# Rotary attention gated by a mixture-scaled sign layer: scales, weight sums and the first loads in another order

## The chip, the core and the metric

The kernel runs on one core of a Trainium2 chip. The core has five engines with queues of their own: TensorE (PE in the profile, with its weight loads apart as PEld), VectorE (DVE), ScalarE (ACT), GpSimd (POOL) and SyncE (SP), which here does nothing but issue transfers. They meet at semaphores. Matmul results land in PSUM, everything else lies in SBUF. The metric is the device time of one execution in microseconds (us), the median of the runs; all tensors are float32.

## What is computed

Cut to what matters (B = 4 sequences of S = 512 tokens, E = 1024, 16 heads of 64, NE = 8 experts):

```python
xn = layernorm(x)                                   # over E, eps 1e-5
q, k, v = xn @ Wq, xn @ Wk, xn @ Wv                 # rotary on q and k
attn = softmax(mask(q @ k.T) / 8)                   # causal
s = (attn @ v) @ Wo
routing = softmax(xn @ gate_w.T)                    # (tokens, 8)
in_scale = routing @ in_channel_scale               # (8, 1024)
out_scale = routing @ out_channel_scale
f = ((xn * in_scale) @ sign(weight).T) * out_scale + bias
out = x + s * silu(f)
```

The two channel scales are tables of 8 rows and 1024 columns. The kernel multiplies them by the routing on TensorE in the format float32r, with each value split into a high part (rounded to float32r) and a low part (the value less the high part). Partition rows of the tables `isc` and `osc` hold groups of eight experts; of each 16 rows eight keep the high part and eight the low part.

## The kernel before

**Stages.** Normalized x is transposed into `X[b]` (features on partitions), one sequence at a time. The projections run in 16 slots, one for each sequence b and group g of four heads (`project`, three matrices m = 0, 1, 2 for q, k, v). Each projection is a Strassen-Winograd product: seven block products in place of eight, over sums and differences of the weight (`form_w`, S1 to S4, VectorE, line 253) and of x (`form_x`, T1 to T4, line 265). A slot is 84 steps of `project`, some 28 for each m. Between these steps the attention of the group before is interleaved in pieces: transposes of the probabilities (`transpose_p`, into `pT`), `scores_1`, `scores_3`, `scores_02`, and `values` (product with v). After the slots come the sign layer (`ffn`, line 874), with which the last attention units are interleaved, and the output projection (`project_out`, line 994), again with a Strassen form. Its sums of the weight Wo (`sum_wo`, line 865) are made once, while the first two `ffn` groups run: t1 to t4, each in four pieces c.

**Order.** TensorE runs in the order in which the program is written (`manual_schedule` for PE). VectorE and ScalarE are in written order in the beginning only (the loop over four tiles, lines 693 to 719); elsewhere a planner orders each engine's queue at compile time by when it reckons that inputs are there.[...] `tc.keep_in_program_order` pins an instruction behind the instruction that was written last for its engine ahead of it; others may still be put between. SP's transfers are in a planned order as well, and all go through one queue.

**Beginning.** Four tiles of x (512 KB each, `load_x`) and the first weight in two halves (`load_half_w`, 512 KB each) are loaded in the order tile 0, tile 1, half 0, tile 2, tile 3, half 1. For each tile VectorE takes statistics (line 179), ScalarE the deviation (187), VectorE the reciprocal and the normalized tile (194, 195), TensorE transposes (209). TensorE runs filler transposes (`keep_warm`, line 669) while it waits. The statistics of tile t + 1 stand ahead of the normalization of tile t in VectorE's queue.

**Interleaving.** `interleave` runs the pieces of a slot evenly over the 84 steps. In slot 0 there is no attention yet; its nine pieces are the three steps of the router (`router`: logits, softmax, transposed result `rt` at line 547), the loads of the scales, their splitting, and empty ones:

```python
            while done * len(pieces) < (n + 1) * n_fill:
                next(fill, None)
                done += 1
```

**Scales.** `load_scales` fills the 128 rows of a tile by 16 transfers of the same eight rows (line 563). `split_scales` makes `is_high` from a mask (568, 569), rounds the tile on ScalarE (572), subtracts on VectorE (573), clears the low part where the row is a high one (574), and puts both together (575). The two tiles come from the pool `xin`, whose two buffers take the tiles of the next sequence afterwards (line 169).

**The end of the attention.** The last two units u0 and u1 are transposed in three steps each, with a step of `ffn` after each (`dense`), and then multiplied by v (`values`). `dense(gates, 5)` takes a weight sum after each of its steps; two more are taken after each `values`. PSUM banks for all of this come from one ring of four (`bank`).

Of the kernel before, what the change touches and what calls it, by code (L numbers as in the profile page):

```python
# [9 lines left out]
F32 = mybir.dt.float32  # L10
F32R = mybir.dt.float32r
AF = mybir.ActivationFunctionType
ALU = mybir.AluOpType
AX = mybir.AxisListType
# [8 lines left out]
NE = 8  # L23
P = 128
# [21 lines left out]
def t_place(h, j):  # L46

    return [(h, 0), (2 + h, 0), (4, 256 * h), (2 + h, 384)][j]
# [3 lines left out]
def attn_gated_ffn_kernel(  # L52
# [14 lines left out]
    nc = tc.nc  # L67
# [3 lines left out]
    cp = ctx.enter_context(tc.tile_pool(name="const", bufs=1))  # L71
# [9 lines left out]
        out=mask,  # L81
        in_=mask,
# [17 lines left out]
    isc = cp.tile([P, E], F32R, name="isc")  # L100
    osc = cp.tile([P, E], F32R, name="osc")

    high = cp.tile([P, 8], F32, name="high")
    nc.gpsimd.memset(high, 1.0)
    for sign, base in ((1, 0), (-1, 7)):
        nc.gpsimd.affine_select(
            out=high,
            in_=high,
# [3 lines left out]
            pattern=[[-16 * sign, 8]],  # L112
            channel_multiplier=sign,
        )
    is_high = cp.tile([P, 2], F32, name="is_high")

# [34 lines left out]
    def bank(name):  # L153
        return ring.tile([P, S], F32, tag="r", name=name)
# [9 lines left out]
    def load_x(b, t):  # L164
        if b == 0:
            xt = X1[:, t, :]
        else:
            xt = xip.tile([P, E], F32, tag="x", name=f"x_{b}_{t}")
        nc.sync.dma_start(out=xt, in_=x[(b * TPB + t) * P : (b * TPB + t + 1) * P, :])
        xin[b, t] = xt  # L170
# [26 lines left out]
    def layernorm(b, t):  # L197
        half_statistics(b, t, 0)
        half_statistics(b, t, 1)
        deviation(b, t)  # L200
        normalize(b, t)
# [274 lines left out]
    def values(u):  # L476
        b, g, i = u
        pr = g + NGRP * i
        pv = bank("pv_%d_%d_%d" % u)
        for j in range(TPB):  # L480
            for h in range(2):
                r = h * D
                n, o = t_place(h, j)
                nc.tensor.matmul(  # L484
                    pv[r : r + D, j * P :],
                    lhsT=V[u][:, j, r : r + D],
                    rhs=PT[u][:, n, o : o + (TPB - j) * P],
                    start=(j == 0),
                    stop=(j == TPB - 1),
                )  # L490
        at = atp.tile([P, S], F32, tag="at", name="at_%d_%d_%d" % u)
        nc.vector.tensor_copy(at, pv)
        nc.sync.dma_start(
            out=at_d[b].rearrange("t p (c q) -> p t c q", c=NC)[:, :, pr, :],
            in_=at.rearrange("p (t q) -> p t q", t=TPB),
        )
# [54 lines left out]
                nc.sync.dma_start(out=rt_d[b, t], in_=rT[32 * t : 32 * t + 32, :])  # L551


    staged, scales = {}, []

    def load_sign(n):
        staged[n] = xip.tile([P, E], F32, tag="x", name=f"wb_{n}")
# [1 line left out]

    def load_scales(src):  # L560
        v = xip.tile([P, E], F32, tag="x", name="scales")
        for t in range(P // NE):
            nc.sync.dma_start(out=v[NE * t : NE * (t + 1), :], in_=src)
        scales.append(v)

    def split_scales(dst):
        v = scales.pop(0)
        nc.vector.tensor_reduce(is_high[:, 0:1], high, AX.X, ALU.max)
        nc.vector.tensor_scalar(
            is_high[:, 1:2], is_high[:, 0:1], -1.0, 1.0, op0=ALU.mult, op1=ALU.add  # L570
        )
        nc.scalar.copy(dst, v)
        nc.vector.tensor_tensor(v, v, dst.bitcast(F32), op=ALU.subtract)
        nc.vector.tensor_scalar(v, v, is_high[:, 1:2], None, op0=ALU.mult)
        nc.vector.scalar_tensor_tensor(
            dst, dst.bitcast(F32), is_high[:, 0:1], v, op0=ALU.mult, op1=ALU.add
        )

    def make_sign(n):
# [97 lines left out]
    def load_half_w(i):  # L677
        nc.sync.dma_start(
            out=W[0, 0, 0][:, i].rearrange("p c n -> p (c n)"), in_=wqkv[0, 0][:, i * E : (i + 1) * E]
        )  # L680

    load_half_w(0)
    load_x(0, 2)
    load_x(0, 3)
    load_half_w(1)
    nc.sync.dma_start(out=gw[:, :, :NE], in_=gate_wT.rearrange("(c p) e -> p c e", p=P))
# [34 lines left out]
    def attention_pieces(k, late):  # L721

        units = [(*groups[k], i) for i in range(2)]
        w, v = late

        def pt(u):
            return [lambda n=n: transpose_p(u, n) for n in range(5)] if u else []

        def with_values(scores_of, u):
            def both():  # L730
                scores_of(units)
                if u:
                    values(u)

            return both

        def wait():
            pass

        pieces = [  # L740
            *pt(w),
            with_values(scores_1, w),
            *pt(v),
            with_values(scores_3, v),
            wait,
            lambda: scores_02(units),
            wait,
            wait,
        ]
        return pieces, units  # L750
# [12 lines left out]
    for k, (b, g) in enumerate(groups):  # L763
        pieces = []
        if k > 0:
            pieces, late = attention_pieces(k - 1, late)
        extra = []
        if g == 0:
            routing = [lambda n=n: router(b, n) for n in range(3)]
            if k == 0:  # L770
                nothing = lambda: None
                pieces = [
                    routing[0],
                    lambda: (load_scales(in_scale), load_scales(out_scale)),
                    routing[1],
                    nothing,
                    routing[2],
                    nothing,
                    lambda: split_scales(isc),
                    lambda: split_scales(osc),  # L780
                    nothing,
                ]
            else:

                pieces.insert(7, routing[0])
                pieces.insert(10, routing[1])
                pieces.insert(13, routing[2])
        elif g == 1 and b + 1 < B:
            for t in range(2):
                load_x(b + 1, t)  # L790
        elif g > 1 and b + 1 < B:
            t0 = 2 * (g - 2)
            for t in range(t0, t0 + 2):
                layernorm(b + 1, t)
            extra = [
                lambda t=t, h=h: transpose_x(b + 1, t, h) for t in range(t0, t0 + 2) for h in range(2)
            ]
            if g == 2:
                extra.append(lambda: [load_x(b + 1, t) for t in (2, 3)])

        step = max(1, (len(pieces) + len(extra)) // (len(extra) + 1))
        for n, e in enumerate(extra):
            pieces.insert(min(len(pieces), (n + 1) * step + n), e)
        if k in (4, 8, 12, 13):
            n = {4: 0, 8: 2, 12: 4, 13: 6}[k]
            pieces.insert(8, lambda: make_sign(n + 1))
            pieces.insert(4, lambda: make_sign(n))
            pieces.insert(0, lambda: (load_sign(n), load_sign(n + 1)))
        if b == B - 1:

            if g < 2:
                load_xn(g)
            if g in (1, 2):
                pieces.insert(3, lambda: in_scales(g - 1, score_banks))
            if g == 3:
                z_place[0] = [xip.tile([P, E], F32, tag="x", name=f"z0_{i}") for i in range(2)]
                pieces.insert(3, lambda: out_scales(0, score_banks))
        fill = project(b, g) if k else first
        interleave(pieces, fill, 3 * 7 * 4)
        if g == NGRP - 1 and b + 1 < B:  # L820
            for n in (3, 1, 2, 4):
                form_x(b + 1, n)
# [17 lines left out]
    for f, k in ((0, 1), (0, 0), (1, 1), (1, 0)):  # L840
        w = wop.tile([P, 4, HALF], F32, name=f"wo{f}{k}")
        for n in range(2):
            nc.sync.dma_start(
                out=w[:, 2 * n : 2 * n + 2, :].rearrange("p c n -> p (c n)"), in_=wo[k, 2 * f + n]
# [12 lines left out]
    def sum_wo(n, c):  # L857
        out_, x0, x1 = {
            1: (t1, b12, b11),
            2: (t2, b22, t1),  # L860
            3: (t3, b22, b12),
            4: (t4, b21, t2),
        }[n]
        tc.keep_in_program_order(
            nc.vector.tensor_tensor(out_[:, c, :], x0[:, c, :], x1[:, c, :], op=ALU.subtract)
        )
# [45 lines left out]
    u0, u1 = units = [(*groups[-1], i) for i in range(2)]  # L912
    w, v = late
    sums = iter([(n, c) for n in (1, 3) for c in range(4)])

    def dense(gates, n):
        for _ in range(n):
            next(gates)
            if n > 1:
                nxt = next(sums, None)  # L920
                if nxt:
                    sum_wo(*nxt)
# [7 lines left out]
    gates = gated(0)  # L930
# [13 lines left out]
    split(1, 1)  # L944
    scores_02(units)
    gates = gated(1)
    dense(gates, 5)

    sums = iter([(n, c) for n in (2, 4) for c in range(4)])
    dense(gates, 5)  # L950
    for u in units:
        for ns in ((0, 1), (2, 3), (4,)):
            for n in ns:
                transpose_p(u, n)
            dense(gates, 1)
        values(u)
        for nxt in [next(sums, None) for _ in range(2)]:
            if nxt:
                sum_wo(*nxt)
    for _ in gates:  # L960
        pass
    actx.close()
# [190 lines left out]
```

## Time and profile before

| | |
|---|---|
| time, median of 3 runs | 1192.41 us (1191.88 to 1192.67) |
| profiled execution: time | 1192.43 us |
| profiled execution: span | 1190.7 us |
| mean granted TensorE clock | 0.997 |
| HBM read, written | 95.45 MB, 25.43 MB: 102 GB/s over the span |
| first slot ends | about 54.5 us |
| last projection slot ends | about 842 us |
| output projection begins | 898.8 us |

The span runs from the first to the last instruction that the profile shows. A row of waits names the waiting engine, tile and line, then what ended the wait. In a timeline row, the brackets give the engine's idle time just before the instruction and what ended it. The chain is followed back from the last instruction to what released each step. In the windows the columns are length, busy time and instructions of PE, PEld, DVE, ACT and POOL, then the granted TensorE clock (1.00 is full), the busy share of the DMA engines and their GB/s.

### The profile page before, as it was taken

How to read it: one execution, taken by the hardware profiler on the slowest of the kernel's cores; microseconds unless marked ns; L12 is line 12 of the kernel's file. 1: busy time of each engine (PE TensorE's matmuls, PEld its weight loads, DVE VectorE, ACT ScalarE, POOL GpSimd, SP SyncE). 2: the span in 40 equal slices, each digit the busy share in tenths (PEclk: the TensorE clock that was granted, in tenths of full speed). 3: DMA queues.
4: the chain of work that ended last, by engine and by line, in shares of the span. 5: the costliest groups of instructions: out<-in, count | busy, mean ns of one | idle time of the engine just before them, and what ended most of it. 6: DMA issues, size and time to landing. Idle time of an engine off the chain costs nothing.

```text
span 1190.7 us, 17943 instructions
## 1 busy us (share of the span) xinstructions
PE 1174.0 (99%) x6760; PEld 895.1 (75%) x6760; DVE 760.6 (64%) x1397; ACT 492.3 (41%) x1133; POOL 536.5 (45%) x597
## 2 busy tenths in 40 slices
PE   8989999999999999999999999999999999999998
PEld 7869788888878888887978888887774456645664
DVE  7667676875767686576768677666865533453343
ACT  2534646443564645455463544446532121222120
POOL 0453436353433635343453544255465445544544
PEclk9989999999999999999999999999999999999999
DMA  8422432421133242223235222210504523432320
GB/s 286 142 63 72 133 107 80 151 83 56 70 115 116 89 133 72 74 81 115 85 120 203 65 80 80 80 50 18 210 9 145 194 77 107 146 102 79 107 71 35
DMA packets 60246, 122.04 MB, mean 102 GB/s; under 512 B 5248, under 2 KB 40832, under 8 KB 54144
## 3 DMA queue, kind: packets, MB, share of 16 engines
q1 hardware_dynamic: 55296, 112.11, 29.0%
q0 software_dynamic: 4576, 8.39, 2.0%
q8 instruction: 53, 0.87, 0.3%
q10 hardware_dynamic: 288, 0.39, 0.1%
q14 instruction: 33, 0.27, 0.1%
HBM read 95.45 MB, written 25.43 MB: 102 GB/s over the span
## 4 chain that ended last, share of the span: by engine, by line
PE 94%; DVE 3%; ACT 1%; DMA 1%; issue 0%; POOL 0%; SPq 0%; ACTq 0%; DVEq 0%
PE pj L304 33%; PE wo L994 16%; PE pj L312 16%; PE ff L874 9%; PE sc L402 6%; PE pv L484 6%; PE ptp L468 6%; PE xtp L209 1%; DVE nmx L417 1%; ACT p L420 1%; PE lg L506 1%; DMA x<-in_x 1%; DVE sc L413 0%; PE os L652 0%; PE is L624 0%
## 5 line engine op out<-in xcount | busy, mean ns | idle before, releaser
L430 POOL TENSOR_SCALAR p<-p,rs 128x128 f32<-128x128 f32 (+3 forms) x256 | 167.9, 669 | 182.5 <-DVE rs L428 182.5
L420 ACT ACTIVATE p<-sc,nmx 128x128 f32<-128x128 f32 (+3 forms) x256 | 132.8, 524 | 163.1 <-DVE nmx L417 160.6
L304 PE MATMUL pj<-T,S 128*128 128x256 f32 x768 | 185.0, 384 | 6.1 <-DVE S L253 6.1
L304 PEld LDWEIGHTS pj<-T,S 128*128 128x128 f32 x768 | 141.3, 192 | 25.0 <-issue 7.7
L366 POOL TENSOR_TENSOR part<-part,part 128x256 f32<-128x256 f32 x48 | 35.0, 728 | 211.4 <-ACT part L365 181.3
L276 POOL TENSOR_TENSOR sw<-sw,sin_sb 128x512 f32<-128x512 f32 x64 | 85.6, 1337 | 90.2 <-ACT sw L274 90.2
L304 PE MATMUL pj<-X,w 128*128 128x256 f32 x512 | 123.0, 381 | 0.2 <-ACT X L215 0.2
L474 ACT COPY pT<-ptp 128x512 f32<-128x512 f32 x96 | 56.2, 586 | 125.6 <-PE ptp L468 125.0
L417 DVE TENSOR_REDUCE nmx<-sc 128x2 f32<-128x512 f32 (+3 forms) x128 | 103.5, 819 | 2.6
L874 PE MATMUL ff<-sg,hi 128*128 128x512 f32 x256 | 103.3, 404 | 0.0
L304 PEld LDWEIGHTS pj<-X,w 128*128 128x128 f32 x512 | 92.7, 190 | 12.1 <-issue 1.1
L874 PE MATMUL ff<-sg,lo 128*128 128x512 f32 x256 | 99.9, 390 | 0.0
L253 DVE TENSOR_TENSOR S<-w 128x512 f32<-128x512 f32 x96 | 78.4, 818 | 30.8 <-PE pj L304 27.0
L468 PE MATMUL ptp<-ident,p 128*128 128x128 f32 x640 | 94.9, 273 | 3.0 <-DVE pT L472 1.6
L312 PE MATMUL pj<-S,T 128*128 128x128 f32 x768 | 92.9, 277 | 0.0
L273 ACT ACTIVATE sw<-c 32x512 f32<-32x512 f32 x128 | 80.4, 628 | 30.0 <-DVE c L331 28.0
L468 PEld LDWEIGHTS ptp<-ident,p 128*128 128x128 f32 x640 | 78.6, 141 | 18.1 <-DVE pT L472 2.0
L312 PEld LDWEIGHTS pj<-S,T 128*128 128x128 f32 x768 | 88.3, 192 | 2.2 <-issue 0.5
L277 POOL TENSOR_TENSOR rot<-rot,sw 128x512 f32<-128x512 f32 x64 | 83.0, 1297 | 4.9
L402 PE MATMUL sc<-rot,rot 64*128 64x384 f32 (+3 forms) x512 | 82.0, 449 | 0.0
L274 ACT ACTIVATE sw<-c 32x512 f32<-32x512 f32 x128 | 80.4, 628 | 1.8
L484 PE MATMUL pv<-pT,v 128*64 128x256 f32 (+3 forms) x512 | 76.0, 439 | 0.0
(141 smaller groups left out, 1997.6 us busy)
## 6 DMA issues: line engine op xcount, KB each, us to landing
w<-in_wqkv SPq DMA_DIRECT2D x47, 1024.0 KB
x<-in_x SPq DMA_DIRECT2D x16, 512.0 KB
xn_d<-X SPq DMA_DIRECT2D x16, 512.0 KB
at_d<-at SPq DMA_DIRECT2D x32, 256.0 KB
xp<-xn_d SPq DMA_DIRECT2D x16, 512.0 KB
ap<-at_d SPq DMA_DIRECT2D x16, 512.0 KB
xr<-in_x SPq DMA_DIRECT2D x16, 512.0 KB
wb<-in_wb SPq DMA_DIRECT2D x8, 512.0 KB
```

Source lines behind the costliest of these rows:

```text
L276: nc.gpsimd.tensor_tensor(sw, sw, sin_sb, op=ALU.mult)
L277: nc.gpsimd.tensor_tensor(rot, rot, sw, op=ALU.add)
L304: nc.tensor.matmul(ps, lhsT=wq[:, k, :], rhs=xq[:, k, :], start=(k == 0), stop=(k == 3))
L312: nc.tensor.matmul(ps[:, j * P : (j + 1) * P], lhsT=xq[:, k, j * P : (j + 1) * P], rhs=wq[:, k, :], start=(k == 0), stop=(k == 3),)
L402: nc.tensor.matmul(ps[:, h, :], lhsT=Q[u][r : r + D, i * P : (i + 1) * P], rhs=K[u][r : r + D, : (i + 1) * P], start=True, stop=True,)
L417: nc.vector.tensor_reduce(nmx, ps, AX.X, ALU.max, negate=True)
L420: nc.scalar.activation(pt[:, h, :], ps[:, h, :], AF.Exp, bias=nmx[:, h : h + 1], accum_out=ssum[:, h : h + 1],)
L430: nc.gpsimd.tensor_scalar(pt[:, h, :], pt[:, h, :], rs[:, h : h + 1], 1.0, op0=ALU.mult, op1=ALU.mult,)
L468: nc.tensor.transpose(tp[:, k, :], probs(u, i)[:, h, j * P : (j + 1) * P], ident)
L484: nc.tensor.matmul(pv[r : r + D, j * P :], lhsT=V[u][:, j, r : r + D], rhs=PT[u][:, n, o : o + (TPB - j) * P], start=(j == 0), stop=(j == ...
L874: nc.tensor.matmul(acc, lhsT=part[q, i][:, c, :], rhs=sg[4 * k + c // 2][:, (c % 2) * HALF : (c % 2 + 1) * HALF], start=(c == 0 and part i ...
L994: nc.tensor.matmul(ps, lhsT=lhs[:, k, :], rhs=rhs[:, k, :], start=(k == 0), stop=(k == 3))
```

## The change

Four edits that don't depend on one another:

1. The host repeats the eight rows 16 times, so that each scale is one transfer of 512 KB. The split is done on VectorE alone, all of it pinned: a copy that rounds, a multiplication by the low mask, and one operation `dst * sign + v` with sign +1 on high rows and -1 on low ones. The masks are made once. In slot 0 the splits move from pieces 7 and 8 to pieces 4 and 6, each behind a step of the router (counted from 1).
2. Tile 2 of the first sequence is loaded ahead of the first half weight.
3. A slot with more than 18 pieces gets one empty piece at its end (before the pieces for sign weights are put in).
4. The sums t2 and t4 of Wo leave the second `dense` and the places after `values`: three pieces of t2 go between the transposes of u1, the last piece of t2 and all of t4 behind the values of u1.

```diff
-    is_high = cp.tile([P, 2], F32, name="is_high")
+    row_kind = cp.tile([P, 3], F32, name="row_kind")
...
-    staged, scales = {}, []
+    staged, scales, scales_done = {}, [], []
...
     def load_scales(src):
         v = xip.tile([P, E], F32, tag="x", name="scales")
-        for t in range(P // NE):
-            nc.sync.dma_start(out=v[NE * t : NE * (t + 1), :], in_=src)
+        nc.sync.dma_start(out=v, in_=src)
         scales.append(v)
 
     def split_scales(dst):
         v = scales.pop(0)
-        nc.vector.tensor_reduce(is_high[:, 0:1], high, AX.X, ALU.max)
-        nc.vector.tensor_scalar(
-            is_high[:, 1:2], is_high[:, 0:1], -1.0, 1.0, op0=ALU.mult, op1=ALU.add
-        )
-        nc.scalar.copy(dst, v)
-        nc.vector.tensor_tensor(v, v, dst.bitcast(F32), op=ALU.subtract)
-        nc.vector.tensor_scalar(v, v, is_high[:, 1:2], None, op0=ALU.mult)
-        nc.vector.scalar_tensor_tensor(
-            dst, dst.bitcast(F32), is_high[:, 0:1], v, op0=ALU.mult, op1=ALU.add
+        h, low, sign = (row_kind[:, n : n + 1] for n in range(3))
+        pin = tc.keep_in_program_order
+        if not scales_done:
+            pin(nc.vector.tensor_reduce(h, high, AX.X, ALU.max))
+            pin(nc.vector.tensor_scalar(low, h, -1.0, 1.0, op0=ALU.mult, op1=ALU.add))
+            pin(nc.vector.tensor_scalar(sign, h, 2.0, -1.0, op0=ALU.mult, op1=ALU.add))
+        scales_done.append(dst)
+
+        pin(nc.vector.tensor_copy(dst, v))
+        pin(nc.vector.tensor_scalar(v, v, low, None, op0=ALU.mult))
+        pin(
+            nc.vector.scalar_tensor_tensor(
+                dst, dst.bitcast(F32), sign, v, op0=ALU.mult, op1=ALU.add
+            )
         )
...
+    load_x(0, 2)
     load_half_w(0)
-    load_x(0, 2)
     load_x(0, 3)
     load_half_w(1)
...
                     routing[0],
                     lambda: (load_scales(in_scale), load_scales(out_scale)),
                     routing[1],
+                    lambda: split_scales(isc),
+                    routing[2],
+                    lambda: split_scales(osc),
                     nothing,
-                    routing[2],
                     nothing,
-                    lambda: split_scales(isc),
-                    lambda: split_scales(osc),
                     nothing,
...
             pieces.insert(min(len(pieces), (n + 1) * step + n), e)
+        if len(pieces) > 18:
+
+            pieces.append(lambda: None)
         if k in (4, 8, 12, 13):
...
     gates = gated(1)
-    dense(gates, 5)
-
-    sums = iter([(n, c) for n in (2, 4) for c in range(4)])
-    dense(gates, 5)
+    dense(gates, 10)
     for u in units:
         for ns in ((0, 1), (2, 3), (4,)):
             for n in ns:
                 transpose_p(u, n)
             dense(gates, 1)
+            if u == u1:
+                sum_wo(2, ns[0] // 2)
         values(u)
-        for nxt in [next(sums, None) for _ in range(2)]:
-            if nxt:
-                sum_wo(*nxt)
+    sum_wo(2, 3)
+    for c in range(4):
+        sum_wo(4, c)
     for _ in gates:
...
-        "in_scale": np.ascontiguousarray(a["in_channel_scale"]),
-        "out_scale": np.ascontiguousarray(a["out_channel_scale"]),
+        "in_scale": np.tile(a["in_channel_scale"], (P // NE, 1)),
+        "out_scale": np.tile(a["out_channel_scale"], (P // NE, 1)),
```

## The prediction, made before the result was known

> **What bounds the kernel now.** I read the page's busy rows first, then TensorE's own waits, then the chain that ended last around the longest of them, then windows for the granted clock.
>
> The page, busy time and share of the span:
>
> ```profile
> PE 1174.0 (99%) x6760; PEld 895.1 (75%) x6760; DVE 760.6 (64%) x1397; ACT 492.3 (41%) x1133; POOL 536.5 (45%) x597
> ```
>
> TensorE (PE) is the bound: 16.7 us of the 1190.7 us span are left beside it, and its order is written by hand, so a microsecond in which it stands still is a microsecond of the kernel. No other edit can pay than one that takes away such a stop or a slow clock. TensorE's waits (us in total, times, longest):
>
> ```profile
> PE pj L304 <- DVE S L253: 6.1, 1, 6.1
> PE ptp L468 <- DVE pT L472: 1.6, 1, 1.6
> PE idle L669 <- POOL ident masks.py:199: 1.5, 1, 1.5
> PE xtp L209 <- DVE x L195: 1.3, 2, 1.0
> PE ptp L468 <- POOL p L430: 1.0, 2, 0.5
> ```
>
> One wait of 6.1 us stands out. The chain of waits in order of time (start, us, what) shows what made it:
>
> ```profile
> 60.18 0.94 ACT osc L572
> 61.15 1.34 DVE scales L573
> 62.52 0.76 DVE scales L574
> 63.31 1.28 DVE osc L575
> 64.59 0.61 DVE S L253
> 65.20 0.14 issue
> 65.34 5.04 PE pj L304 x12
> 70.38 1.92 PE sc L402 x8
> ```
>
> The form S3 of group (0,1) needs 0.6 us of VectorE, but stands in its queue behind the split of `osc`, which waits for ScalarE's cast. The transfer isn't to blame: weight 0,1,0 was issued at 33.71, and the DMA rate falls from 377 to 29 GB/s by 38. TensorE stands from 59.20 to 65.34, and then its twelve matmuls take 5.04 us; at full clock twelve take 2.60 (the chain has eight of them in 1.73 wherever it is undisturbed). The windows give the clock (column after the five engines):
>
> ```profile
> 62.00:64.00 2.00, 0.00 (x0) 0.00 (x0) 1.93 (x3) 0.00 (x0) 2.00 (x5) 0.75 0.20 33
> 64.00:66.00 2.00, 0.66 (x2) 0.60 (x3) 1.97 (x4) 0.00 (x0) 1.99 (x4) 0.50 0.40 70
> 66.00:68.00 2.00, 2.00 (x6) 1.58 (x5) 1.55 (x3) 0.00 (x0) 0.00 (x0) 0.50 0.82 277
> 68.00:70.00 2.00, 2.00 (x7) 1.58 (x5) 0.69 (x1) 0.00 (x0) 0.00 (x0) 0.54 0.08 14
> ```
>
> So the stall costs 6.14 us and a half clock after it: 4.97 (65.34 to the scores' 70.31) - 2.60 = 2.37. Together **8.51 us**.
>
> **Part by part. Scales.** 32 transfers of 32 KB become two of 512 KB: the same bytes, 30 issues fewer on SP. In before these fill SP's queue from 20.63 to 33.60, and weight 0,1,0 goes out directly after, at 33.71; it can now go a few us sooner. The two big transfers stand behind a queue that is full until about 24.5 (over 300 GB/s until there) and add at most 1 MB, about 3 us at that rate, so I estimate both landed by 28; the first split comes at about 32 and the second at 41.5 (below). Hidden, with 4 us or more of cover; without it, VectorE stands on the transfer.
>
> The split loses its ScalarE cast (1.04 each) and the subtraction (1.23 and 1.33), and gains a VectorE copy and one tiny operation. The copy isn't in the trace. Its lower end is the scalar multiply of the same tile, 0.75; its upper end that row's other instance, 1.64. The whole split is 0.75 + 0.75 + 1.28 = 2.8 us without and 1.64 + 1.64 + 1.96 = 5.2 with GpSimd beside it; the first has 0.45 of tiny operations more.[...] 1.64 at 49.81, while GpSimd ran `sw` and `rot`, 0.75 at 62.52.[...] I use the row, 5.2, as the worst.
>
> Where do they stand? The interleaving puts the first split at step 36 of 84 (four products into m = 1, behind the first `rot`s on VectorE, 32.1 in before's time) and the second at step 55 (behind c[1] at 41.5). TensorE's next needs of VectorE are the router's `rt` at 37.39 (1.4 us of tiny operations before it) and a bank at about 40. At 3.2: 32.1 + 3.2 + 1.4 = 36.7, in time; with GpSimd[...] (its rows run from 34.08) 32.1 + 5.7 + 1.4 = 39.2, a stop of 1.8. Part of the split is over before 34.08, so I take nothing, 1.8 as the end. The second split moves the `rot`s from 43.03 to about 46; their GpSimd addition of the last pair ran at 50.98 and the scores at 54.49, so it is covered. Before's first split already held VectorE from 48.55 to 53.67 while TensorE ran 12.50 us of `pj` L312 without a stop: cover of that kind exists.
>
> What comes after the stall goes? With no split behind 56, S3 needs only its weight and u3, both there by 51 without the split. In the next slot the same form ran at 99.20, eleven us ahead of its product at 109.86. If the planner leaves S3 behind the second reciprocal (60.22, there was no more than that ahead of the split), TensorE waits until about 61.15, 1.95 us, and not long enough for the clock: the 1.57 us wait at 886 left it at 1.00. I take zero.
>
> [...] the row has 4.97 us at half, 2.37. I take the row.
>
> **The third tile.** The beginning runs on the input's arrival:
>
> ```profile
> 2.20 7.52 DMA x<-in_x
> 9.75 0.69 DVE bn L179
> ...
> 11.50 0.64 PE xtp L209 x4
> ```
>
> Tile 2 lands at 9.72 behind half a weight; VectorE waits 1.10 for it, and normalizing tile 1 stands behind that. One 512 KB transfer ahead less, at 400 GB/s of these windows, is 1.3 us: landed at about 8.4, when VectorE comes free. Also the two `is_high` operations (6.56 to 6.89), now pinned in the split, leave the queue ahead of the first reciprocal: 0.25. VectorE ends tile 1 at 10.13, TensorE is through its fourteen fillers at 10.23, so the transposes start at 10.25, not 11.50: **1.25 us**, all of it kept down the chain (xtp, copy, pj, deviation, xtp, lg, pj at 20.63 all hang on it). The half weight lands at 9.7 instead; its product then starts at 11.55 (12.80), so 1.8 us of cover. Tile 3 and the second half are in the same place of the queue (estimate 11.1 and 12.5), asked for at 10.9 and 13.6. Ends: 0.8 if tile 2 comes at 8.85, 1.35.
>
> **The extra piece.** Lists of over 18 pieces (groups 2, 3, 4, 6, 7, 8, 10, 11, 12: nine slots) get an empty one at the end, so later pieces come some three steps of 0.43 us sooner, 1.3 us. The two 0.5 us waits on `p` L430 (265.12, 476.38) are the first transposes behind groups 4 and 8; their chain from the scores at 257.57 to GpSimd's end moves 1.3 ahead: **1.0 us**. It costs VectorE and ScalarE nothing in instructions; last copies of `pT` end 2.1 (117.15 against 119.25) and 2.9 us ahead of their `pv`, more than the step or two lost.
>
> **Weight sums.** Five L865 subtractions leave the stretch 879 to 887. There (start, us, VectorE and PE):
>
> ```profile
> 885.15 1.76 DVE L865 TENSOR_TENSOR z_t<-wo,xp 128x512 f32<-128x512 f32 x1
> ...
> 886.84 1.28 DVE L472 COPY pT<-ptp 128x512 f32<-128x512 f32 x2
> 887.57 0.66 PE L468 MATMUL ptp<-ident,p 128*128 128x128 f32 x4 [1.57 <-DVE pT L472]
> ```
>
> The copies come next after z_t (883.85), two us sooner: **1.57 us**. The sums go behind the last transposes: three singles of 0.68 between them, and five at the end, 3.4 us behind `at` (899.51 in before). VectorE was idle from 900.8 to 906.06 there, 5.3; `t2` is needed at 905.79, `t4` at 916.09. Covered; if GpSimd stretched all five to 1.76, 8.8 us would push the first `c` L1004 some 3, and TensorE has three more banks before it waits.
>
> **Sum.** 8.51 + 1.25 + 1.0 + 1.57 = 12.33. The profiled execution took 1192.43 (span 1190.7), the median is 1192.41: the same. 1192.4 - 12.3 = **1180.1 us**.
>
> **Rivals.** (a) S3 stays behind the second reciprocal: 1.95 back, 1182.1. For: in before it stood behind everything of that stretch. Against: the next slot. (b) The first split holds the router: 1.8 back, 1181.9[...]. For: GpSimd's rows at 34 to 39.7. Against: it starts before them. (c) The beginning is held by tile 3 or the half weight: nothing of 1.25, 1181.4. (d) The change doesn't do what it says: the planner still holds the form behind work that late, and 8.5 stays: 1188.6. (e) **Slower**: the squeezed pieces bring transposes onto banks whose copies wait behind ScalarE's four `sw` copies (0.63 each), one stop in each of nine slots. At the size of the one such stop in the trace, 1.57, that is 14.1, 1180.1 + 1.0 + 14.1 = 1195.2; it decides from 1.26 us a slot (11.3 / 9). Against: no such stop in any of these slots now, 2.1 us of slack.
>
> **Numbers.** Forecast 0.62, (a) 0.13, (b) 0.12, (c) 0.07, (d) 0.02, (e) 0.04. The range 1178.3 to 1185: below, the upper ends (1.35, the 0.2 and 0.3 of other small waits) and half a us of spread; above, (a), (b) and (c) two at a time. It leaves out (d), (e) and the end of (b), under 1 in 10 by these chances; the rest is room for a new order of the planner that no row shows. 0.2% (2.4 us) is about what a measurement of this kernel can tell from no change. Faster 0.95, within 0.01, slower 0.04.
>
> **What would show it.** Right: no wait on S L253 and a clock of 1.00 from 55 to 75; `xtp` for tile 1 at about 10.25; no `ptp` waits on POOL p; no wait at `pT` L472 near the end. Wrong: a wait of `rt` L547 or `pj` on VectorE at 35 to 45, or TensorE waits repeated in the nine slots.

## The result, and the profile after

| | before | after |
|---|---|---|
| median of 4 runs, us | 1192.54 (1191.88 to 1192.91) | 1179.76 (1179.35 to 1180.39) |
| ratio to before, 95% interval | | 0.9894 [0.9877, 0.9911] |
| profiled execution: time, span | 1192.43, 1190.7 | 1179.35, 1177.6 |
| mean granted TensorE clock | 0.997 | 0.999 |

The time fell by 12.8 us in the medians and by 13.1 in the profiled executions; 12.3 was predicted. The busy row of the page after, and TensorE's longest waits (us in total, times, longest):

```profile
PE 1170.6 (99%) x6760; PEld 893.5 (76%) x6760; DVE 754.0 (64%) x1396; ACT 489.3 (42%) x1131; POOL 535.4 (45%) x597
```

```profile
PE idle L673 <- POOL ident masks.py:199: 1.5, 1, 1.5
PE ptp L468 <- DVE v L331: 0.3, 1, 0.3
PE xtp L209 <- DVE x L195: 0.3, 1, 0.3
PE pj L304 <- ACT X L215: 0.2, 1, 0.2
PE rt L547 <- DVE rex L543: 0.2, 1, 0.2
```

The waits on `S` L253, on `pT` L472 and on `p` L430 are gone, and with them all that was longer than 0.3 us behind the start. One entry is new: the router's `rt`, 0.2. The same stretch as the half clock of before, in the windows after:

```profile
55.00:60.00 5.00, 5.00 (x25) 4.41 (x24) 2.68 (x7) 2.31 (x9) 0.93 (x2) 1.00 0.21 90
60.00:65.00 5.00, 5.00 (x23) 3.16 (x22) 3.78 (x5) 1.13 (x3) 1.36 (x2) 1.00 0.00 2
65.00:70.00 5.00, 5.00 (x25) 4.41 (x24) 3.56 (x9) 2.13 (x7) 4.29 (x5) 1.00 0.30 77
```

TensorE is busy throughout, and the clock (behind the five engines) is 1.00. The form S3 that it had waited for now runs at about 46.6.

Where the time came from is read best from starts: take the same instruction in both traces, and see by how much it is earlier. That lead grows in four places and shrinks in one.

| place | lead, from and to | step, us | predicted |
|---|---|---|---|
| beginning (`pj` at 20.63 before, 19.37 after) | 0 to 1.26 | 1.26 | 1.25 |
| router's `rt` | 1.26 to 0.82 | -0.44 | 0 |
| stall and half clock in slot 1 | 0.82 to 9.40 | 8.58 | 8.51 |
| the two stops on `p` | 9.40 to 10.83 | 1.43 | 1.0 |
| end of the attention | 10.89 to 13.06 | 2.17 | 1.57 |

The sum is 13.0. The last unit's end after, VectorE's rows (start, us, line, operation):

```profile
879.52 0.69 DVE L472 COPY pT<-ptp 128x512 f32<-128x512 f32 x1 [0.38 <-PE ptp L468]
880.13 0.68 DVE L872 TENSOR_TENSOR xp<-wo,xp 128x512 f32<-128x512 f32 x1
881.26 0.69 DVE L472 COPY pT<-ptp 128x512 f32<-128x512 f32 x1 [0.45 <-PE ptp L468]
...
888.47 2.49 DVE L872 TENSOR_TENSOR z_t<-wo,xp 128x512 f32<-128x512 f32 x4
893.00 0.69 DVE L1010 TENSOR_TENSOR c<-wo,part 128x512 f32<-128x512 f32 x1 [2.04 <-PE wo L1000]
```

Each copy of `pT` now waits for its transposes, not they for it. The single sums (L872; the third runs at 884.27) come behind the copies, and those moved to the end are through 2.04 us before the first result of the output projection is there.

### The profile page after: what moved, and what is told of

Its sections match the earlier page's. It is cut to its first block, busy times and chain, and to the rows that moved or that the text cites. A ratio compares the mean times of both kernels' runs of the same rounds, so it can differ in the third digit from the quotient of the medians.

```text
span 1177.6 us, 17904 instructions
## 1 busy us (share of the span) xinstructions
PE 1170.6 (99%) x6760; PEld 893.5 (76%) x6760; DVE 754.0 (64%) x1396; ACT 489.3 (42%) x1131; POOL 535.4 (45%) x597
## 4 chain that ended last, share of the span: by engine, by line
PE 98%; DVE 1%; ACT 0%; issue 0%; POOL 0%; DVEq 0%; ACTq 0%; POOLq 0%
PE pj L304 33%; PE pj L312 17%; PE wo L1000 16%; PE ff L881 10%; PE sc L402 7%; PE pv L484 6%; PE ptp L468 6%; PE xtp L209 1%; PE idle L673 1%; PE lg L506 1%; PE os L656 0%; PE is L628 0%; DVE z_t L1025 0%; DVE nmx L417 0%; ACT p L420 0%
## 5 line engine op out<-in xcount | busy, mean ns | idle before, releaser
L430 POOL TENSOR_SCALAR p<-p,rs 128x128 f32<-128x128 f32 (+3 forms) x256 | 167.4, 667 | 212.9 <-DVE rs L428 194.7
L304 PE MATMUL pj<-T,S 128*128 128x256 f32 x768 | 182.3, 380 | 0.0
L253 DVE TENSOR_TENSOR S<-w 128x512 f32<-128x512 f32 x96 | 77.4, 806 | 27.4 <-PE pj L304 23.9
```

Of the source, the lines that this page charges most:

```text
L304: nc.tensor.matmul(ps, lhsT=wq[:, k, :], rhs=xq[:, k, :], start=(k == 0), stop=(k == 3))
L430: nc.gpsimd.tensor_scalar(pt[:, h, :], pt[:, h, :], rs[:, h : h + 1], 1.0, op0=ALU.mult, op1=ALU.mult,)
```

## The experiments

Twelve kernels ran. The names b_ are the kernel before with one part added, the names a_ the changed kernel with one part taken back or altered. The kernel before was run beside each lot, with medians of 1192.29, 1192.12 and 1192.48.

| kernel | median, us (lowest to highest) | ratio to before, 95% interval |
|---|---|---|
| b_one_transfer | 1190.26 (1187.89 to 1191.56) | 0.9982 [0.9976, 0.9989] |
| b_vector_split | 1187.92 (1187.57 to 1188.04) | 0.9962 [0.9947, 0.9977] |
| b_early_pieces | 1192.07 (1191.52 to 1193.67) | 0.9999 [0.9990, 1.0007] |
| b_pinned | 1187.42 (1186.44 to 1188.17) | 0.9958 [0.9943, 0.9972] |
| a_old_tile_order | 1180.29 (1180.29 to 1180.90) | 0.9902 [0.9886, 0.9919] |
| a_no_piece | 1181.51 (1181.12 to 1182.25) | 0.9911 [0.9897, 0.9926] |
| a_old_sums | 1182.74 (1181.91 to 1182.98) | 0.9920 [0.9905, 0.9935] |
| a_splits_behind_router | 1179.90 (1179.67 to 1180.31) | 0.9898 [0.9883, 0.9912] |
| a_32_fillers | 1179.00 (1179.00 to 1179.06) | 0.9889 [0.9874, 0.9904] |
| a_22_fillers | 1178.99 (1178.84 to 1180.25) | 0.9891 [0.9876, 0.9906] |
| a_32_old_tile_order | 1180.29 (1179.97 to 1180.52) | 0.9900 [0.9884, 0.9917] |
| a_late_places | 1180.21 (1179.88 to 1180.64) | 0.9899 [0.9885, 0.9914] |

### Which part of the first edit removes the stall

**One transfer alone.**

```diff
-        for t in range(P // NE):
-            nc.sync.dma_start(out=v[NE * t : NE * (t + 1), :], in_=src)
+        nc.sync.dma_start(out=v, in_=src)
```

> Before, with each scale in one transfer and nothing else changed: the split keeps its cast on ScalarE and its late pieces. Theory P (the planner reckons 32 transfers ahead of weight 0,1,0 and so puts the form S3 late in VectorE's queue; their number alone decides): the 6.1 us wait on S L253 and the half clock go, 8.5 us, 1184.0 us. Rival S (the split's late place and its cast hold the form): the wait stays, 1192.5 us. Rival T (the weight itself comes late behind the 32 issues): also 1184.0 us.

The wait on `S` L253 is gone, but 2.0 us were gained and not eight. TensorE's longest wait, and the chain of waits of this kernel (start, us, what):

```profile
PE rt L547 <- DVE is_high L567: 4.2, 1, 4.2
```

```profile
21.04 6.77 DMA scales<-in_out_scale
27.81 0.02 issue
27.83 0.04 ACT osc L571
27.88 0.91 issue
28.79 0.37 ACT part L365
...
33.07 1.13 DVE scales L572
34.21 0.09 DVE rrs L530
34.30 1.17 DVE isc L574
35.47 1.21 DVE rex L531
...
37.01 1.00 DVE rhi L536
...
38.61 1.27 DVE rex L539 x2
...
40.30 0.83 DVE rex L543
...
41.28 0.45 PE rt L547
```

The planner put the split, which nothing pins here, well ahead: VectorE's part of the first one, at 48.55 to 53.67 before, now lies between 27.9 and 35.5. ScalarE stood on the transfer of the second scale until 27.83, ahead of `part` that VectorE needed, and VectorE's part of both splits lay between the router's operations. So the router's last operations came at 35.4 to 41.1, while GpSimd ran four operations for the rotary (34.63 to 41.09). The router's took 1.21, 1.00, 1.27 (a pair) and 0.83 us here, 4.3 together; before they had taken 0.8 together and been through by 33.4, ahead of GpSimd's rows. That stretch of 3.5 us is most of the wait: TensorE stood 4.2 us for `rt`, and from 40 to 45 the clock was 0.50. The stall was moved, not removed.

The twenty runs of this kernel differ by 3.7 us, and their mean clock from 0.996 to 1.000. The fastest, 1187.89, is the only one at 1.000. Only one of them has a trace.

**The split on VectorE alone**, pinned, with 32 transfers and the late pieces:

```diff
-        nc.scalar.copy(dst, v)
-        nc.vector.tensor_tensor(v, v, dst.bitcast(F32), op=ALU.subtract)
...
+        pin(nc.vector.tensor_copy(dst, v))
+        pin(nc.vector.tensor_scalar(v, v, low, None, op0=ALU.mult))
```

> Before, with the split on VectorE alone and pinned, but 32 transfers and the late pieces. P: the form still stands behind the second reciprocal of the next slot's scores, but no longer behind the split: a wait of 1.5 to 2.0 us on S L253[...] (1.00 throughout), some 6.5 us faster than before with 0.25 from the beginning: 1186 us. S: no wait at all, 1183.8 us. T: the wait stays about 6 us, 1192.5 us.

TensorE's wait is what rival (a) of the prediction said, and the windows show that the clock fell all the same (they are cut where the clock changed, at 62.02 and 65.43):

```profile
PE pj L304 <- DVE S L253: 1.9, 1, 1.9
```

```profile
58.61:62.01 3.40, 1.49 (x8) 1.02 (x7) 2.31 (x5) 1.28 (x5) 2.03 (x4) 1.00 0.00 0
62.02:65.42 3.40, 3.40 (x9) 2.41 (x8) 3.40 (x5) 0.00 (x0) 3.40 (x6) 0.50 0.13 22
65.43:68.84 3.41, 3.41 (x15) 1.74 (x14) 3.14 (x6) 0.11 (x1) 1.81 (x4) 1.00 0.84 202
```

S3 stood directly behind the second reciprocal, ahead of the late `osc` split. The stop ended at 61.24 and the half clock began at 62.02; the twelve matmuls took 4.60 us in place of 2.60, so 1.9 us of stop cost 3.9. This is less than the 8.5 of before by 4.6, and the time fell by 4.4.

**The places alone.**

```diff
                     routing[1],
-                    nothing,
+                    lambda: split_scales(isc),
                     routing[2],
-                    nothing,
-                    lambda: split_scales(isc),
                     lambda: split_scales(osc),
+                    nothing,
+                    nothing,
```

> Before, with only the places of the splits in slot 0 moved to pieces 4 and 6. P and T: nothing changes, 1192.5 us, the wait of 6.1 us stays, since the transfers are as many. S: most of the 8.5 us goes, 1184 to 1186 us.

No difference, and the same wait of 6.1 us. A place in the written program that nothing pins is not a place in VectorE's queue: the planner left that order as it was.

**A pin alone**, with the cast still on ScalarE: the second split's subtraction, and the first mask addition of the scores, are pinned behind the forms.

```diff
-        nc.vector.tensor_tensor(v, v, dst.bitcast(F32), op=ALU.subtract)
+        pin(nc.vector.tensor_tensor(v, v, dst.bitcast(F32), op=ALU.subtract))
...
+            if not scored:
+                tc.keep_in_program_order(added)
```

> Before, with 32 transfers, late pieces and the cast on ScalarE, but the second split and the first scores pinned on VectorE, so that the forms of group 0,1 stand ahead of both. P: the weight has long landed, so S3 runs at about 55.5, the wait on S L253 is gone and the clock stays 1.00: 1184 us. T: S3 waits for its transfer, and TensorE still stands 4 us or more: 1190 us or later.

S3 ran at 55.24 with 32 small transfers still in place, so its weight was not late. But the scores now stood behind the split, and TensorE behind the scores. Both windows below hold a part of that stop, and the clock stayed at 1.00:

```profile
PE sc L404 <- ACT p L425: 2.5, 1, 2.5
```

```profile
60.90:64.30 3.40, 1.88 (x8) 0.68 (x6) 3.17 (x8) 1.15 (x5) 0.93 (x2) 1.00 0.50 154
64.31:67.71 3.40, 2.46 (x11) 1.55 (x12) 2.62 (x5) 1.99 (x7) 0.93 (x2) 1.00 0.00 0
```

**Both parts, late places:** the changed kernel with the splits back at pieces 7 and 8.

```diff
                     routing[1],
-                    lambda: split_scales(isc),
+                    nothing,
                     routing[2],
+                    nothing,
+                    lambda: split_scales(isc),
                     lambda: split_scales(osc),
                     nothing,
-                    nothing,
-                    nothing,
```

> The changed kernel with the splits back at pieces 7 and 8: one transfer for each scale and the pinned split by VectorE alone, without the earlier places. Theory Q, what took the stall away is that nothing of the split waits (no cast on ScalarE, data long landed), so that it is through before the form is due: no wait on S L253, a clock of 1.00 from 55 to 75, none at rt, 1179.9 within 0.5. Rival E, the early places did it: a wait of 1 to 2.5 us on a form or on scores between 54 and 66, 1181 to 1184.

1180.2, no stall and a clock of 1.00. So one transfer and the pinned split by VectorE alone suffice together, and the early places are not needed; either part alone gained only 2.0 or 4.4 us. Against a_splits_behind_router (below), where both splits stand earlier, it loses some 0.4 between 60 and 65, in which TensorE was busy for 4.89 of 5 us. The split ends nearer to the scores here; that this is the reason is not shown.

### The other three edits, each taken back

**The extra piece.**

```diff
-        if len(pieces) > 18:
-            pieces.append(lambda: None)
```

> The changed kernel without the empty piece. Theory W, a wait row shows what a stop costs: two stops of 0.5 on p L430 come back, 1179.8 + 1.0 = 1180.8. Theory F, a stop costs some 0.2 us more than its row[...] (start to start 2.45 in place of 1.79): 1179.8 + 1.43 = 1181.2. Rival N, the piece gave nothing and the two waits went with the earlier edits: 1179.8, no wait on p L430.

```profile
PE ptp L468 <- POOL p L430: 1.0, 2, 0.5
```

The two waits are back with the same row. From 19.64 (19.37) on, where the beginning had cost 0.27, the same `pj` stretch starts at 293.45 (292.46) and 504.71 (503.01): 0.72 for the first stop, 0.71 for the second, together 1.43. The row says 0.5 for each. The size that theory F gave was right. Part of the reason is how a row counts: its idle time begins at the modelled end of the last matmul. In this kernel's first stop the starts were 0.77 us apart (255.22 and 255.99) where 0.11 is usual.

**The weight sums.**

```diff
-    dense(gates, 10)
+    dense(gates, 5)
+    sums = iter([(n, c) for n in (2, 4) for c in range(4)])
+    dense(gates, 5)
...
-            if u == u1:
-                sum_wo(2, ns[0] // 2)
```

> The changed kernel with the sums of Wo in their old places. Theory W, the row of 1.57 us on pT L472 is the cost: 1179.8 + 1.57 = 1181.3. Theory F, two stops come back there, one of 1.57 and one that no row of the list shows, 2.15 by starts: 1181.9. Both expect the wait row on pT L472 again, and the output projection's start after the last pv at the same distance as now.

```profile
PE ptp L468 <- DVE pT L472: 1.6, 1, 1.6
```

The output projection starts at 889.29 in place of 885.83. Of these 3.46, 1.22 came from the beginning (`pj` at 20.59 in place of 19.37, explained below); 2.24 are the sums'. Theory F said 2.15, the row alone 1.57.

**The third tile.**

```diff
-    load_x(0, 2)
     load_half_w(0)
+    load_x(0, 2)
```

> The changed kernel with tile 2 of x behind the first half weight again (is_high stays out of the beginning). Theory P: of the 1.25 us that the beginning gained, 1.0 was the transfer's and 0.25 the two mask operations'. The transposes of tile 1 start at 11.25 in place of 10.25, and the time is 1179.8 + 1.0 = 1180.8. Rival R1, the mask operations gave nothing: they start at 11.50, 1181.0. Rival R2, what the beginning gained is given back in the first slot by a transfer or by the router: under 0.3 more, 1180.0.

The transposes of tile 1 started at 11.12, 0.87 later than after's 10.25, but the medians differ by 0.5. That fits none of the expectations well, and the same number varied in kernels whose beginning was the same: 10.25, 10.51, 11.15, 11.46 and 11.52 with tile 2 first (after, a_no_piece, a_splits_behind_router, a_old_sums, a_late_places). That spread of 1.3 us is as large as the effect. The next experiments went after it.

### The first split and the router

Both splits behind the router's last step:

```diff
                     routing[1],
-                    lambda: split_scales(isc),
+                    nothing,
                     routing[2],
+                    lambda: split_scales(isc),
                     lambda: split_scales(osc),
-                    nothing,
```

> The changed kernel with both splits behind the router's last step (pieces 6 and 7 in place of 4 and 6). Theory B, the first split shares VectorE with the router's last step and costs TensorE 0.44 us at rt L547: the wait of 0.22 there is gone and the time is 1179.8 - 0.4 = 1179.4, with no wait on S L253 and a clock of 1.00 from 55 to 75. Rival L, behind the router the two splits together hold the rot additions or the form S3: a wait of 1.5 to 2 us between 45 and 62, 1181.5. Rival N, rt waits for its softmax anyway: 1179.8.

In the changed kernel the first split runs between the router's operations. VectorE's rows (the last two are the router's, which took 0.29 and about 0.15 in before; GpSimd ran from 32.82 on here), and then TensorE's:

```profile
31.16 0.67 DVE L575 CAST isc<-scales 128x1024 fp32r<-128x1024 f32 x1
...
31.86 0.75 DVE L576 TENSOR_SCALAR scales<-scales,row_kind 128x1024 f32<-128x1024 f32 x1
...
32.64 1.28 DVE L578 SCALAR_TENSOR_TENSOR isc<-isc,row_kind,scales 128x1024 fp32r<-128x1024 f32 x1
33.85 1.36 DVE L539 TENSOR_TENSOR rex<-rex,rhi 128x32 f32<-128x32 f32 x2
...
35.55 0.91 DVE L543 COPY rex<-rhi 128x32 f32<-128x32 f32 x1
```

```profile
36.52 0.33 PE L547 MATMUL rt<-ident,rex 128*128 128x128 f32 x1 [0.22 <-DVE rex L543]
```

With the splits behind the router this wait is gone: from the `pj` at 20.27 to the one behind `rt` at 37.31 are 17.04 us, against 17.48 (19.37 to 36.85) in the changed kernel. That is the expected 0.44, and it stays to the end. But the median didn't show it, because this execution had begun 0.90 late, at 20.27.

### What makes the beginning vary

The chain of waits of the changed kernel begins so:

```profile
1.54 6.24 PE idle L673 x42
7.78 0.90 PE xtp L209 x8
8.68 1.54 PE idle L673 x14
10.22 0.03 issue
10.25 0.64 PE xtp L209 x4
```

and that of a_splits_behind_router, with tile 1 at 11.15:

```profile
1.53 7.17 PE idle L673 x42
```

It is the fillers, not the input. The 42 of them take 6.24 us here and 7.17 there; at the pace of the fourteen (1.54, 0.11 each) they would take 4.6. Their starts are 0.21 us apart at first and 0.11 later. The change of pace comes where the trace's record of the granted clock begins: at 4.53 in the changed kernel, and at 7.40 in b_vector_split, the latest. Ahead of its first entry the record has nothing, and the windows show 1.00; that is why the column doesn't show the slow pace. Tile 1 follows the change. The change came at 4.53, 5.11, 6.42, 7.05 and 7.19 in the five kernels listed under the third tile, and tile 1 at 10.25, 10.51, 11.15, 11.46 and 11.52. With tile 2 early, the normalized tile 0 is there at about 7.6 and stands behind late fillers.

So ten fillers were taken out of the version above:

```diff
-    keep_warm(42)
+    keep_warm(32)
```

> The changed kernel with both splits behind the router, and 32 fillers in place of 42 ahead of the first tile. Theory F, the beginning waits for the fillers: in the ten traces so far they end at 7.8 to 9.2, since TensorE runs them at half pace (0.22 us each) until somewhere between 4.8 and 7.6 and at 0.11 afterwards, while the first normalized tile is there by about 7.6. Ten fewer end at 6.7 to 8.1: the transposes of tile 1 start at 10.1 to 10.5 in every execution, and the time is 0.4 to 0.9 under the same kernel with 42 (1179.9), so 1179.0 to 1179.5. Rival C, with the fillers gone TensorE stands still, the pace stays at half or falls again, and the fourteen fillers behind tile 0 take 3.1 in place of 1.54: tile 1 at 11.6 or later, 1180.3 or more.

Tile 1's transposes start at 10.28, and the four runs lie within 0.06 us, at 1179.00; the changed kernel's spread over 1.0. The waiting is now TensorE's own for `x`, as it should be (0.55 us at 7.62). This is 0.8 under the changed kernel's median and 0.9 under that of the same version with 42. By ratios of separate lots this is less than can be told apart (0.06%), but the beginnings and the spread show it. Four equal runs don't prove that it is always so: in a_32_old_tile_order (below) the pace changed at 7.34, the same 32 fillers took 6.53 us, and the transposes of tile 0 began at 7.90 in place of 7.62.

> The same with 22 fillers. They end at about 5.9 to 6.4 and TensorE stands for 1.2 to 1.7 us ahead of the first tile. Theory F alone: the same beginning as with 32, 1179.0 to 1179.5. Rival C: the pace isn't at full by then, or falls back; the transposes and the fourteen fillers run at half pace, tile 1 at 11.6 or later, 1180.3 or more.

Three of four runs were as fast (1178.84 to 1179.05); the profiled one took 1180.25. TensorE's wait and windows there:

```profile
PE xtp L209 <- DVE x L195: 2.2, 2, 1.9
```

```profile
4.55:7.96 3.41, 1.53 (x14) 1.29 (x13) 3.34 (x7) 0.29 (x1) 0.00 (x0) 1.00 0.94 320
7.97:11.37 3.40, 3.40 (x18) 3.40 (x17) 3.08 (x8) 1.36 (x3) 0.00 (x0) 0.50 1.01 358
```

A stop of 1.88 us, and the clock at half behind it: the fourteen fillers took 2.73. Rival C's cost is there in this execution, theory F's time in the other three; 22 is too few to rely on.

With 32 fillers, tile 2 behind the half weight again:

> The kernel with 32 fillers and splits behind the router, with tile 2 behind the first half weight again. Without the fillers in the way the transfer's own effect is left. Theory P: tile 1 at 11.1 to 11.3 (held by tile 2's arrival at 9.1 to 9.7), 0.8 to 1.0 over a_32_fillers. Rival N, the order of the tiles gives nothing: no difference.

Tile 1 at 11.32 in place of 10.28, and 1180.29 against 1179.00. With fewer fillers in the way, the order of the tiles is worth the 1.0 that was argued from the transfer (in the profiled executions; 1.3 in the medians).

## Why the prediction was right, point by point

**The stall (8.51, measured 8.58).** Right, with the half clock behind it counted by the row (2.37): it lasted from 62.99 to 69.82, and 4.48 us of it fell on work. The experiments say more than the prediction did of how: neither one transfer nor the new split alone gives it, because one brings a wait at `rt`, the other leaves the form behind the reciprocal. The prediction took the early places for part of the mechanism; they are not.

**"In time for `rt`" (taken as 0, measured 0.44).** The split was as short as estimated (0.67 + 0.75 + 1.28 = 2.7), but it wasn't ahead of the router: they ran mixed, and the router's last operations fell into GpSimd's rows: a pair that took 0.29 before took 1.36, and one of about 0.15 took 0.91. The value lies between the ends given, 0 and 1.8; zero was wrong.

**The price of the copy.** Between 0.75 and 1.64 had been taken; in the changed kernel it ran in 0.67 and 0.68, and where the splits stood late it took up to 1.75 (a_late_places, at 49.89). The upper ends of the longer operations were too low as well: behind the router the multiplication took 2.50 at 46.01 (1.64 was taken), while a multiplication of GpSimd ran from 46.65 to 47.95, and the last operation took 2.46 in a_late_places (1.96 was taken). The 2.50 is more than the longest row of this operation in before, 1.64; what made it so long is not shown. It cost no wait of TensorE's there.

**The third tile (1.25, measured 1.26 in the profile).** The number is right by luck. The step that failed is "TensorE is through its fourteen fillers at 10.23": that is the end of the fillers where the slow pace ends early, and in other traces it was up to 11.5. The runs show 0.5 between the medians with and without the edit, and 1.0 to 1.3 once the fillers are fewer.

**The extra piece (1.0, measured 1.43) and the weight sums (1.57, measured 2.17 and 2.24).** Both mechanisms were right; the size was read from the rows of waits. By the lead from start to start a stop of 0.5 was 0.7 and the one of 1.57 was 1.8; a second stop just ahead of it was 0.4 (ending at 883.99 in before), a row of 0.2 that had not been counted. Together these are 1.0 more than predicted, of which `rt` took 0.44 back. So the sum came nearer to the result than its terms did. No late stop took their place: the sums at the end were covered, and none of the nine slots of rival (e) has a new wait.

**Rival (a)'s price.** "Not long enough for the clock" was wrong: the 1.9 us stop of b_vector_split did lower it and cost 3.9, so that rival should have stood at up to 1184, not 1182.1. The longer stop of b_pinned, 2.47 us, left it at 1.00 (last section).

## What to carry to other kernels

A stall behind work that waits for another engine went away here only when that work had its data early and waited for no other engine. One of the two alone left a stop of 4.2 or 1.9 us, pinning the order alone one of 2.5, and moving the call in the program changed nothing. Price a stop of the bounding engine from start to start, against the same stretch without the stop: here the row of the wait was the lower figure (0.5 against 0.7, 1.57 against 1.8), and with the half clock behind it a stop of 1.9 cost 3.9. And fillers ahead of an engine's first work are instructions in its queue: count how long they take at the slow pace (here 0.21 us from start to start, 0.11 later), and end them before the first real work is due.

## What the runs showed of the hardware that was not expected

- **In these traces the clock went with TensorE's busy time in windows of 3.41 us, not with the length of one stop.** The traces record each change of the granted clock. In all fourteen the times between changes are whole multiples of 3.413 us: 58.03 (17 of them) and 6.83 (2) in before, 54.61 (16) and 3.41 (1) in b_vector_split. Counted in such windows from the first change:

| kernel, stop | window | TensorE busy in it, us | clock in the next window |
|---|---|---|---|
| before, 6.14 us | 59.58 to 62.99 | 0.00 | 0.50 |
| the same | 62.99 to 66.41 | 1.07 | 0.50 |
| b_vector_split, 1.91 us | 58.60 to 62.02 | 1.51 | 0.50 |
| a_22_fillers, 1.88 us | 4.55 to 7.96 | 1.53 | 0.50 |
| before, 1.57 us near the end | 885.61 to 889.02 | 1.85 | 1.00 |
| b_pinned, 2.47 us | 60.89 to 64.30 | 1.89 | 1.00 |
| the same | 64.30 to 67.72 | 2.47 | 1.00 |

  The longer stop of b_pinned, behind which the clock stayed at 1.00, fell into two windows, 1.52 and 0.94 us; each shorter one in the table lay in a single window. Over all windows of the fourteen traces, each with 1.53 us of work or less was followed by a clock of 0.50, and none that ran at 1.00 with 1.85 us or more was. At half clock or at the fillers' slow pace none with 2.45 us or less was followed by 1.00 or the full pace (b_vector_split, 0.57 to 3.99, counted back from its first change), and each with 2.99 or more was (the changed kernel, 1.11 to 4.53). What lies between these limits no run shows, and TensorE's busy time is modelled. The half clock of before, which cost 2.37 us, lasted for two such windows: the one from 62.99 had 1.07 us of work, and 0.50 followed; the one from 66.41 had 3.41, and 1.00 followed.

- **Where a stop falls against these windows differs from execution to execution.** The first change lies between 4.53 and 7.40 us in the fourteen traces, and the later ones come whole multiples of 3.413 us behind it. The mean clock of b_pinned was 1.000 in two runs (1186.44 and 1186.91 us) and 0.998 in the two others (1188.17 and 1187.93). The first of them alone has a trace; that in the two longer ones the stop lay in one window fits, but is not shown.
- **The fillers' slow pace ended where the first change is recorded.** In the changed kernel their starts are 0.21 us apart until 4.36 and 0.11 from 4.56 on, with the change at 4.53. The 42 fillers took 6.24 to 7.65 us in these traces, and the transposes of tile 1 came 10.25 to 11.52 us in with the same order of loads. The four runs of the changed kernel spread over 1.0 us; with 32 fillers it was 0.06 in four runs.
